# A transformer block on one core: the queue's products as halves of 64 rows between attention scores

## The chip, the cores and the metric

The kernel runs on one core of a Trainium2 chip. The metric is the device time of one launch in microseconds, inputs and outputs in the chip's main memory. Engines are called TensorE (PE), VectorE (DVE), ScalarE (ACT), GpSimd (POOL) and SyncE (SP, here the queue that issues transfers). TensorE's array has 128 rows by 128 columns. A matmul with 64 contraction rows uses half of the rows: rows 0 to 63 or rows 64 to 127, by where its operands lie. These halves are called row groups here.

## The reference

One post-norm transformer block over x of 4 x 2048 x 256, all in float32: attention with 16 heads of 16 and a full softmax, a residual and a layer norm, then a gated feed-forward of width 704 whose inputs and weights are rounded to FP4 in blocks of 16, a residual and a layer norm.

```python
scores = einsum('bhld,bhmd->bhlm', q, k) * SCALE
out = einsum('bhlm,bhmd->bhld', softmax(scores), v)
x = layernorm(x + out @ Wo.T)
h = silu(fp4_linear(x, w_gate)) * fp4_linear(x, w_up)
x = layernorm(x + fp4_linear(h, w_down))
```

## The kernel before, in words

**The periods.** The work is cut into steps (b, qb, g): one batch, a block of 512 queries, a group of 4 heads. There are 4 x 4 x 4 = 64 steps, and each runs over 16 key tiles of 128: 1,024 periods. The loop at the end of the kernel goes over periods `n`, from -`LEAD` (-20) to the last. In each it writes out instructions by a string, `ORDER`:

```python
ORDER = "m0 q m1 e0 e1 v e2 e3".split()
```

- `m0`, `m1` (`maxima`): scores of the step that is 20 periods ahead, for two heads each, queries on the output's partitions. Head j of the two lies on rows 64j to 64j+61, so its two matmuls use the two row groups. Both write one PSUM tile of two banks (`pm`), and one VectorE reduction over 128 x 1024 takes the row maxima of both heads (`mx`). After 16 periods `max_rows` turns the maxima and puts their negatives into the last rows of `q`, so that the scores below come out with the maximum subtracted.
- `e0` to `e3` (`exponentials`): the scores of one head and key tile, keys on the partitions, in one bank (`pe`), then ScalarE's exponential into SBUF (`e`, `E_BUFS` buffers).
- `v` (`values`): four matmuls `av`, each with 32 columns of weights (values and a column of ones), for the exponentials of two periods ago (`LAG`). Four such matmuls use the four column strips of the array side by side. At a step's end `normalize` divides by the sums.
- `q` (`more`): one part from a queue of other work: the projections of later blocks (`project`: `ptx` transposes, `pq`, `pv`), the weights' preparation (`prepare`), the output projection, and the feed-forward of the block that has just been attended (`feed_forward`: `py`, `ptq`, `pg`, `pu`, `pth`, `pz`), besides urgent parts of `max_rows` and `normalize` (`pn`, `pa`, `pr`). These parts are Python generators. A part is one PSUM bank's worth of matmuls or transposes and what reads it. Products have 128 contraction rows, and a float32 matmul appears as two rows of the trace; the scores' operands are of a rounded type and appear as one.

**Order.** TensorE's instructions (lines 148 and 151, through helpers) and VectorE's (line 83, `InOrder`) are kept in the order of the source. Whatever waits on TensorE (for a bank that VectorE or ScalarE still reads) stands in front of all that follows.

**PSUM.** There are eight banks: `ps_m` two tiles of two banks for maxima, `ps_av` one, `ps_x` three that exponentials and the queue's parts take in turn.

**Delays.** `later` and `take_due` do small VectorE and GpSimd steps (layer norm, FP4 rounding) a number of periods after they were asked for. A part whose data isn't ready by that count gives its period up.

**Ahead and after.** In the 20 periods ahead of the loop's start only maxima and two parts a period are written. The last block's feed-forward follows the loop in a version of its own (`feed_forward_last`).

Of the kernel before, what the change touches and what calls it, by code (L numbers as in the profile page):

```python
# [54 lines left out]
ORDER = "m0 q m1 e0 e1 v e2 e3".split()  # L56
E_BUFS = 10
LEAST = 300.0
# [17 lines left out]
class InOrder:  # L76
# [5 lines left out]
    def __getattr__(self, name):  # L82
        return lambda *args, **kw: self.tc.keep_in_program_order(getattr(self.engine, name)(*args, **kw))  # L83


@with_exitstack
def block_kernel(
# [25 lines left out]
    ps_m = ctx.enter_context(tc.tile_pool(name="ps_m", bufs=2, space=PSUM))  # L113
    ps_av = ctx.enter_context(tc.tile_pool(name="ps_av", bufs=1, space=PSUM))
    ps_x = ctx.enter_context(tc.tile_pool(name="ps_x", bufs=3, space=PSUM))


    banks = {"n": 0, "more": False}
# [31 lines left out]
    def transpose(*args):  # L150
        tc.keep_in_program_order(nc.tensor.transpose(*args))  # L151

# [107 lines left out]
    def turn_w(name, dst):  # L260
        for kc in range(KC):
            pt = psum("ptw")
            for n in range(KC):
                transpose(pt[:, n * P : (n + 1) * P], loaded[name][:, n, kc * P : (kc + 1) * P], ident)
            if name == "wv":
# [12 lines left out]

    RF = FF // 8

    def prepare():
# [5 lines left out]
        for kc in range(KC):  # L287
            for n in range(KC):
                at = (kc * KC + n) * P
                transpose(pt[:, at : at + P], raw[:, n, kc * P : (kc + 1) * P], ident)  # L290
        nc.scalar.copy(woT.rearrange("p k n -> p (k n)"), pt)
        yield 600
# [10 lines left out]
        def transposed(w, i, q, done):  # L303
            while not done():
                yield LEAST
            if w is w_down:
                q = q.rearrange("p b f -> p (b f)")
                for c0 in range(0, NFC, 4):
                    pt = psum("ptw")
                    for c in range(c0, min(c0 + 4, NFC)):  # L310
                        n = min(P, FF - c * P)
                        at = (c - c0) * P
                        transpose(pt[:n, at : at + P], q[:, c * P : c * P + n], ident)
                        nc.scalar.copy(wdT[:n, c, i * P : (i + 1) * P], pt[:n, at : at + P])
                return
            q = q.rearrange("p (c b) f -> p c (b f)", c=2)
            pt = psum("ptw")
            for kc in range(KC):
                for c in range(2):
                    at = (2 * kc + c) * RF  # L320
                    transpose(pt[:, at : at + RF], q[:, c, kc * P : (kc + 1) * P], ident[:RF, :RF])
# [3 lines left out]
            )  # L325

        pieces = [(w, i) for w in (w_gate, w_up) for i in range(4)] + [(w_down, i) for i in range(KC)]
        q = load(*pieces[0])
        yield 1
        for piece, after in zip(pieces, pieces[1:] + [None]):  # L330
# [3 lines left out]
            yield 600  # L334

    def weave(main, other, k):

        for cost in main:
            yield cost
            for _ in range(k if cost else 0):  # L340
                cost = next(other, None)
                if cost is None:
                    break
                yield cost
# [4 lines left out]
    def project(b, tb, what):  # L349
# [7 lines left out]
        for kc in range(KC):  # L357
            pt = psum("ptx")
            for t in range(QT):
                transpose(pt[:, t * P : (t + 1) * P], xb[:, t, kc * P : (kc + 1) * P], ident)  # L360
            nc.scalar.copy(xT[:, kc, :], pt)
            yield 600

        def q_or_k(name, c):
# [3 lines left out]
            for half in range(2):  # L368
                cols = slice(half * QB // 2, (half + 1) * QB // 2)
                pq = psum("pq")[:, : QB // 2]  # L370
                for kc in range(KC):
                    matmul(pq, w[:, kc, c * P : (c + 1) * P], xT[:, kc, cols], start=(kc == 0), stop=(kc == KC - 1))
                nc.scalar.copy(hi[:, cols], pq)
                nc.gpsimd.tensor_tensor(lo[:, cols], read(pq), hi[:, cols].bitcast(F32), ALU.subtract)
                yield 900
# [8 lines left out]
        def values_of():  # L384
            for t in range(QT):
                v = vt[(tb * 2 + t // 2) % 4]
                pv = psum("pv")
                for kc in range(KC):
                    matmul(
                        pv[:, :D], xT[:, kc, t * P : (t + 1) * P], wvT[:, kc, :], start=(kc == 0), stop=(kc == KC - 1)  # L390
                    )
# [11 lines left out]
                yield 900  # L403
# [35 lines left out]
    def maxima(s, n, i):  # L439

        if n == 0 and i == 0:
            mx_sb[s] = p2.tile([P, QT, HG, NQB], F32, tag="mx", name="mx")
        kb, t = n // QT, n % QT
        pm = ps_m.tile([P, 2, QB], F32, tag="pm", name="pm")
        for j in range(2):
            rows = slice(R * j, R * j + RM)
            matmul(
                pm[:, j, :],
                q_sb[s, i][rows, t * P : (t + 1) * P],
                k_sb[s, i, kb][rows, :],  # L450
                start=True,
                stop=True,
            )
        vector.tensor_reduce(mx_sb[s][:, t, 2 * i : 2 * i + 2, kb], pm, AX.X, ALU.max)

    def max_rows(s):
# [9 lines left out]
        for t in range(QT):  # L466
            transpose(
                pn[: 2 * HG, t * P : (t + 1) * P], nh[:, t].rearrange("p h c -> p (h c)").bitcast(F32), ident
            )
        nr = p2.tile([2 * HG, QB], F32R, tag="nr", name="nr", bufs=1)  # L470
        nc.scalar.copy(nr, pn[: 2 * HG, :])
        for i in range(NP):
# [5 lines left out]
        yield 400  # L478

    def exponentials(s, kt, h):  # L480
        i, j = divmod(h, 2)
        kb, col = kt // QT, kt % QT * P
        pe = psum("pe")
        rows = slice(R * j, R * j + R)
        matmul(pe, k_sb[s, i, kb][rows, col : col + P], q_sb[s, i][rows, :], start=True, stop=True)
        e = p1.tile([P, QB], F32, tag="e", name="e", bufs=E_BUFS)
        nc.scalar.activation(e, pe, AF.Exp, scale=SCALE)  # L487
        e_sb[s, kt, h] = e

    def values(s, kt):  # L490
        if kt == 0:
            av_ps[s] = ps_av.tile([P, QB], F32, tag="av", name="av")
# [11 lines left out]
    def normalize(s):  # L504
# [6 lines left out]
        for t in range(QT):  # L511
            transpose(pa[:, t * P : (t + 1) * P], av_sb[:, t * P : (t + 1) * P], ident)
# [14 lines left out]
        yield 600  # L527
        if s % 2 == 0:
            return
        yield 0  # L530
        pr = psum("pr")
        for t in range(QT):
            transpose(pr[:, t * P : (t + 1) * P], oq_of[s // 2][:, t, :], ident)
        oT = p1.tile([P, QB], F32, tag="oT", name="oT", bufs=3)
        nc.scalar.copy(oT, pr)
        oTs[s // 2] = oT
        yield 600
# [19 lines left out]
    def residual(b, qb, x1, xq):  # L557

        for t in range(QT):
            py = psum("py")  # L560
            for c in range(KC):
                matmul(
                    py[:, :D],
                    oTs[(b * NQB + qb) * KC + c][:, t * P : (t + 1) * P],
                    woT[:, c, :],
                    start=(c == 0),
                    stop=(c == KC - 1),
                )
            nc.gpsimd.tensor_add(x1[:, t, :], x1[:, t, :], read(py[:, :D]))
            if t % 2:  # L570
# [7 lines left out]
            yield 900  # L578

    def gated(xqT, h, t):  # L580
        for half in range(2):
            cols = slice(half * FH, (half + 1) * FH)
            pg = psum("pg")
            for kc in range(KC):
                matmul(
                    pg[:, :FH],
                    xqT[:, kc, t * P : (t + 1) * P],
                    wgT[:, kc, cols],
                    start=(kc == 0),
                    stop=(kc == KC - 1),  # L590
                )
# [4 lines left out]
            nc.scalar.activation(a, pg[:, :FH], AF.Tanh, scale=0.5)  # L596
            nc.gpsimd.tensor_mul(a, a, g)  # L597
            nc.gpsimd.tensor_add(a, a, g)  # L598
            yield 1200
            pu = psum("pu")  # L600
            for kc in range(KC):
                matmul(
                    pu[:, :FH],
                    xqT[:, kc, t * P : (t + 1) * P],
                    wuT[:, kc, cols],
                    start=(kc == 0),
                    stop=(kc == KC - 1),
                )
            u = p2.tile([P, FH], F32, tag="u", name="u")
            nc.scalar.copy(u, pu[:, :FH])  # L610
            nc.gpsimd.tensor_mul(h[:, cols], a, u)  # L611
            yield 1200

    def turned(hq, tiles, hT):
# [4 lines left out]
        for t in range(2):  # L619
            pt = psum("pth")  # L620
            for c in range(4):
                transpose(pt[:, c * P : (c + 1) * P], hq[t][:, c * P : (c + 1) * P], ident)
            nc.scalar.copy(hT[:, t, :4, :].rearrange("p c n -> p (c n)"), pt)
            yield 600
        pt = psum("pth").rearrange("p (t c n) -> p t c n", t=2, c=2)
        for t in range(2):
            for c in range(4, NFC):
                w = min(P, FF - c * P)
                transpose(pt[:w, t, c - 4, :], hq[t][:, c * P : c * P + w], ident)
        for c in range(4, NFC):  # L630
            w = min(P, FF - c * P)
            nc.scalar.copy(hT[:w, :, c, :], pt[:w, :, c - 4, :])
        yield 600

    def down(x1, hT, t):
        for n in range(KC):
            cols = slice(n * P, (n + 1) * P)
            pz = psum("pz")[:, :P]
            for c in range(NFC):
                w = min(P, FF - c * P)  # L640
                matmul(pz, hT[:w, t % 2, c, :], wdT[:w, c, cols], start=(c == 0), stop=(c == NFC - 1))
            nc.gpsimd.tensor_add(x1[:, t, cols], x1[:, t, cols], read(pz))  # L642
            yield 1300

    def feed_forward(b, qb, between):
# [9 lines left out]
        yield from islice(other, 7)  # L655
# [3 lines left out]
        for kc in range(KC):  # L659
            pt = psum("ptq")  # L660
            for t in range(QT):
                q = xq[t // 2][0].rearrange("p (t b) f -> p t (b f)", t=2)
                transpose(pt[:, t * P : (t + 1) * P], q[:, t % 2, kc * P : (kc + 1) * P], ident)
            nc.scalar.copy(xqT[:, kc, :], pt)
            yield 600
# [17 lines left out]
        yield from islice(other, 2)  # L683
        yield from gate(1)
        yield from islice(other, 2)
        yield from gate(2)
        yield from islice(other, 2)
# [18 lines left out]
    def feed_forward_last(b, qb, x1):  # L706
# [4 lines left out]

        def wide(name):
# [18 lines left out]
        def attended(t):  # L731
            py = psum("py")
# [11 lines left out]
        def up(t):  # L744
            pt = psum("ptq")[:, : KC * P].rearrange("p (k n) -> p k n", k=KC)
# [4 lines left out]
            for half in range(2):  # L750
                cols = slice(half * FH, (half + 1) * FH)
                pg, pu = psum("pg"), psum("pu")
# [22 lines left out]
        def downward(t):  # L775
# [3 lines left out]
            for c0 in range(0, NFC, 4):  # L779
                pt = psum("pth")  # L780
# [9 lines left out]
            pz = psum("pz")  # L790
# [183 lines left out]
```

## Time and profile before

| | |
|---|---|
| median of 3 runs | 3632.6 us (3631.36 to 3635.72) |
| the profiled execution | 3627.21 us, span 3625.4 us |
| granted TensorE clock, mean | 0.991 |
| TensorE matmul busy | 3531.5 us |
| VectorE busy | 2859.1 us |
| ScalarE busy | 2677.8 us |
| GpSimd busy | 1248.7 us |

The span is what the trace covers; the profiled execution's own time is 1.8 us over it, and the median 5.4 us over that. TensorE's row counts time in which some matmul's record is open; records overlap, since the next one starts to fetch while the last one still flows through the array. So the time between the starts of two rows tells more than a row's length. `PEld` are weight loads. In a line of the groups stand the engine, the operation, its tiles with shapes and the number of instructions, then the time busy in us, the mean length of one in ns, and the idle time just before them with what ended it.

### The profile page before, as it was taken

How to read it: one execution, taken by the hardware profiler on the slowest of the kernel's cores; microseconds unless marked ns; L12 is line 12 of the kernel's file. 1: busy time of each engine (PE TensorE's matmuls, PEld its weight loads, DVE VectorE, ACT ScalarE, POOL GpSimd, SP SyncE). 2: the span in 40 equal slices, each digit the busy share in tenths (PEclk: the TensorE clock that was granted, in tenths of full speed). 3: DMA queues.
4: the chain of work that ended last, by engine and by line, in shares of the span. 5: the costliest groups of instructions: out<-in, count | busy, mean ns of one | idle time of the engine just before them, and what ended most of it. 6: DMA issues, size and time to landing. Idle time of an engine off the chain costs nothing.

```text
span 3625.4 us, 57726 instructions
## 1 busy us (share of the span) xinstructions
PE 3531.5 (97%) x21348; PEld 1531.6 (42%) x21348; DVE 2859.1 (79%) x3310; ACT 2677.8 (74%) x5446; POOL 1248.7 (34%) x1496
## 2 busy tenths in 40 slices
PE   7889999999999999999999999999999999999997
PEld 5333444443444444444444444434444443434434
DVE  5777888788787877888788888887888788788845
ACT  3667777777777777777777777777777777777772
POOL 1232343423334332343333434333343433233341
PEclk9999999999999999999999999999999999999998
DMA  6533323232232322323223332322332222222200
GB/s 222 168 122 100 103 83 105 85 96 90 90 107 87 110 77 78 112 89 99 90 76 104 96 107 71 110 82 78 106 92 73 64 82 66 64 78 70 68 13 9
DMA packets 190640, 328.39 MB, mean 91 GB/s; under 512 B 24344, under 2 KB 68248, under 8 KB 190360
## 3 DMA queue, kind: packets, MB, share of 16 engines
q1 hardware_dynamic: 188968, 323.39, 29.5%
q8 instruction: 171, 2.80, 0.3%
q10 hardware_dynamic: 1392, 1.31, 0.1%
q14 instruction: 109, 0.89, 0.1%
HBM read 237.04 MB, written 86.51 MB: 89 GB/s over the span
## 4 chain that ended last, share of the span: by engine, by line
PE 88%; DVE 8%; DMA 2%; issue 1%; ACT 1%; SPq 0%; POOL 0%; POOLq 0%; ACTq 0%; DVEq 0%
PE av L148 25%; PE pe L148 19%; PE pm L148 17%; PE pz L148 6%; DVE mx L83 6%; PE pg L148 5%; PE pu L148 5%; PE pq L148 3%; PE pv L148 2%; PE py L148 2%; PE pth L151 1%; PE pa L151 1%; PE pn L151 1%; DVE m L83 1%; DMA wl<-in_L_ffn_w_gate_dram 1%
## 5 line engine op out<-in xcount | busy, mean ns | idle before, releaser
L83 DVE TENSOR_REDUCE mx<-pm 128x2 f32<-128x1024 f32 x2048 | 2456.6, 1221 | 617.9 <-PE pm L148 533.2
L487 ACT ACTIVATE e<-pe 128x512 f32<-128x512 f32 x4096 | 2216.0, 597 | 534.7 <-PE pe L148 522.0
L148 PE MATMUL av<-e,v 128*32 128x512 f32 x8192 | 1095.0, 607 | 3.3 <-DMA v<-vx 3.3
L148 PE MATMUL pe<-q,k 64*128 64x512 f32 x4096 | 1050.1, 458 | 3.7 <-ACT e L487 2.7
L148 PE MATMUL pm<-k,q 62*128 62x512 f32 x4096 | 934.2, 446 | 48.1 <-DVE mx L83 40.9
L148 PEld LDWEIGHTS pe<-q,k 64*128 64x128 f32 x4096 | 482.5, 185 | 947.7 <-ACT e L487 915.3
L148 PEld LDWEIGHTS pm<-k,q 62*128 62x128 f32 x4096 | 409.1, 186 | 339.6 <-DVE mx L83 179.0
L597 POOL TENSOR_TENSOR a<-a,g 128x352 f32<-128x352 f32 x120 | 112.3, 936 | 621.8 <-ACT a L596 621.7
L148 PEld LDWEIGHTS av<-e,v 128*32 128x32 f32 x8192 | 161.7, 108 | 330.0 <-issue 307.2
L178 POOL TENSOR_TENSOR xn<-xn,m 128x704 f32<-128x704 f32 (+2 forms) x100 | 153.3, 1533 | 249.1 <-DVE m L83 206.7
L148 PE MATMUL pz<-wdT,hT 128*128 128x128 f32 (+1 forms) x1488 | 230.6, 297 | 1.5 <-ACT hT L785 1.5
L148 PEld LDWEIGHTS pz<-wdT,hT 128*128 128x128 f32 x1488 | 188.9, 192 | 64.1 <-issue 43.4
L642 POOL TENSOR_TENSOR x<-x,read 128x128 f32<-128x128 f32 x120 | 55.0, 458 | 414.2 <-ACT read L156 404.0
L148 PE MATMUL pg<-wgT,xqT 128*128 128x352 f32 x512 | 186.6, 487 | 1.8 <-ACT xqT L748 1.8
L148 PE MATMUL pu<-wuT,xqT 128*128 128x352 f32 x512 | 185.7, 485 | 0.0
L611 POOL TENSOR_TENSOR h<-a,u 128x352 f32<-128x352 f32 x120 | 112.5, 938 | 138.5 <-ACT u L610 137.9
L179 POOL TENSOR_TENSOR xn<-xn,m 128x704 f32<-128x704 f32 (+2 forms) x100 | 153.3, 1533 | 7.2
L180 POOL TENSOR_TENSOR xn<-xn,sc 128x704 f32<-128x704 f32 (+2 forms) x100 | 126.2, 1262 | 6.4
L148 PEld LDWEIGHTS pg<-wgT,xqT 128*128 128x128 f32 x512 | 87.7, 190 | 75.0 <-issue 44.6
L148 PEld LDWEIGHTS pu<-wuT,xqT 128*128 128x128 f32 x512 | 88.0, 190 | 73.3 <-ACT e L487 37.3
L598 POOL TENSOR_TENSOR a<-a,g 128x352 f32<-128x352 f32 x120 | 114.8, 957 | 9.3
L156 ACT COPY read<-pz 128x128 f32<-128x128 f32 x120 | 31.8, 265 | 112.1 <-PE pm L148 103.6
(114 smaller groups left out, 2279.5 us busy)
## 6 DMA issues: line engine op xcount, KB each, us to landing
k<-kx SPq DMA_DIRECT2D x1024, 128.0 KB
v<-vx SPq DMA_DIRECT2D x64, 768.0 KB
q<-qx SPq DMA_DIRECT2D x256, 124.0 KB
kx<-khi SPq DMA_DIRECT2D x64, 256.0 KB
qx<-qhi SPq DMA_DIRECT2D x64, 256.0 KB
vx<-vt SPq DMA_DIRECT2D x32, 384.0 KB
xb<-in_L_attn_x_dram SPq DMA_DIRECT2D x16, 512.0 KB
kx<-klo SPq DMA_DIRECT2D x32, 256.0 KB
```

The costliest lines, as they stand in the source:

```text
L83: return lambda *args, **kw: self.tc.keep_in_program_order(getattr(self.engine, name)(*args, **kw))
L148: tc.keep_in_program_order(nc.tensor.matmul(*args, **kw))
L151: tc.keep_in_program_order(nc.tensor.transpose(*args))
L156: nc.scalar.copy(t, bank)
L178: nc.gpsimd.tensor_tensor(xn, xn, m, ALU.add)
L179: nc.gpsimd.tensor_tensor(xn, xn, m, ALU.subtract)
L180: nc.gpsimd.tensor_tensor(xn, xn, sc.unsqueeze(2).to_broadcast([p, nb, FB]), ALU.mult)
L487: nc.scalar.activation(e, pe, AF.Exp, scale=SCALE)
L597: nc.gpsimd.tensor_mul(a, a, g)
L598: nc.gpsimd.tensor_add(a, a, g)
L611: nc.gpsimd.tensor_mul(h[:, cols], a, u)
L642: nc.gpsimd.tensor_add(x1[:, t, cols], x1[:, t, cols], read(pz))
```

## The change

1. A product or a transpose of the queue is cut along its contraction rows: `product` and `turn` make a `Part`, a list of calls in which the upper ones (rows 64 to 127) come first and the lower ones (rows 0 to 63) follow. Both halves of a product add up in the same bank; a transpose's halves write 64 columns each. This holds while `split["on"]` is true, from period 0 until the maxima end.
2. The maxima are four steps a period instead of two: one matmul, one bank and one reduction over 128 x 512 for each head (`maximum`).
3. `ORDER` becomes a table with an order for each kind of part, "turn" (transposes), "square" (up to 256 output columns), "wide" (more), "long" (more than two contraction chunks) and "none". A step `u` issues the next upper call and a step `l` the next lower one. In each order all `u` come ahead of `v` and all `l` behind it, so a period's `l` and the next period's `u` stand in one stretch between two `v`.
4. The queue gives at most one part a period (`take_part`); urgent parts go first through `ready`.
5. PSUM banks are kept by number: three for maxima (four until period 0), one for `av`, four that exponentials and parts take from the head of a list and give back when what reads them has been written (`was_read`). The version for the last block goes round all eight.
6. `E_BUFS` is 11 instead of 10.

```diff
-ORDER = "m0 q m1 e0 e1 v e2 e3".split()
-E_BUFS = 10
+ORDER = {
+    "none": "e3 m1 e1 m2 v e2 m3 m0 e0",
+    "turn": "m3 u u u u e0 e2 m1 v m0 e3 e1 l m2 l l l",
+    "square": "u u e0 m2 e3 m0 v e2 m3 e1 l l m1",
+    "wide": "u m0 u e0 e2 m2 v e3 m3 e1 l m1 l",
+    "long": "u u m2 u u u e2 m0 v m3 e0 e1 e3 l l l l m1 l l",
+}
+FIRST = "m0 m1 m2 m3 q q"
+E_BUFS = 11
...
+    banks, banks_m, taken = deque(range(3)), deque(range(3, 7)), {}
+    def bank_of(i, name):
+        return ps.tile([P, 512], F32, tag=f"bank{i}", name=name)
     def psum(name):
-        banks["n"] += 1
-        if banks["more"] and banks["n"] % 2:
-            return ps_m.tile([P, 2, 512], F32, tag="pm", name=name)[:, 0, :]
-        return ps_x.tile([P, 512], F32, tag="px", name=name)
+        i = banks.popleft()
+        taken.setdefault(name, deque()).append(i)
+        return bank_of(i, name)
+    def was_read(name):
+        banks.append(taken[name].popleft())
...
+    def product(out, pairs):
+        kind = "long" if len(pairs) > 2 else "wide" if out.shape[1] > QB // 2 else "square"
+        def rows(h):
+            return [
+                (lhsT[r], rhs[r])
+                for lhsT, rhs in pairs
+                for r in [slice(h * R, min(h * R + R, lhsT.shape[0]))]
+                if r.start < r.stop
+            ]
+        upper = rows(1) if split["on"] else []
+        parts = upper + rows(0) if split["on"] else pairs
...
+    def turn(pairs):
+        calls, upper = [], 0
+        for h in (1, 0) if split["on"] else (None,):
+            for out, t in pairs:
+                n = t.shape[0]
+                r = slice(0, n) if h is None else slice(h * R, min(h * R + R, n))
+                calls.append(lambda out=out, t=t, r=r: transpose(out[:, r], t[r], ident[r, r]))
...
-        pm = ps_m.tile([P, 2, QB], F32, tag="pm", name="pm")
-        for j in range(2):
-            rows = slice(R * j, R * j + RM)
-            matmul(pm[:, j, :], q_sb[s, i][rows, ...], k_sb[s, i, kb][rows, :], ...)
-        vector.tensor_reduce(mx_sb[s][:, t, 2 * i : 2 * i + 2, kb], pm, AX.X, ALU.max)
+        bank = banks_m.popleft()
+        pm = bank_of(bank, "pm")
+        matmul(pm, q_sb[s, i][rows, t * P : (t + 1) * P], k_sb[s, i, kb][rows, :], start=True, stop=True)
+        vector.tensor_reduce(mx_sb[s][:, t, h : h + 1, kb], pm, AX.X, ALU.max)
+        banks_m.append(bank)
...
+        split["on"] = 0 <= n and m < N
+        part, g = take_part() if n >= 0 else (Part("none", []), None)
+        upper, lower = deque(part[: part.upper]), deque(part[part.upper :])
+        order = (ORDER[part.kind] if n >= 0 else FIRST).split()
+        for at, step in enumerate(order):
...
+            elif step == "u" and upper:
+                upper.popleft()()
+            elif (step == "l" or step == "q") and lower:
+                for _ in range(1 if part.upper else len(lower)):
+                    lower.popleft()()
+                if not lower:
+                    part_done(g)
```

More of the change, by code (lines that the diff above doesn't have):

```diff
@@ L333, in prepare, with some @@
             q = following
-            yield 600
-    def weave(main, other, k):
[L338 to L344, printed above, removed]
+    def some(parts, k):
+        while k > 0:
+            part = next(parts, None)
+            if part is None:
+                return
+            yield part
+            k -= part == LEAST
+    def weave(main, other, k):
+        for part in main:
+            yield part
+            if part == LEAST:
+                yield from some(other, k)
         yield from other
@@ L560, in residual @@
             py = psum("py")
[L561 to L568, printed above, removed]
+            yield product(
+                py[:, :D],
+                [(oTs[(b * NQB + qb) * KC + c][:, t * P : (t + 1) * P], woT[:, c, :]) for c in range(KC)],
+            )
             nc.gpsimd.tensor_add(x1[:, t, :], x1[:, t, :], read(py[:, :D]))
+            was_read("py")
             if t % 2:
@@ L583, in gated @@
             pg = psum("pg")
[L584 to L591, printed above, removed]
+            yield product(pg[:, :FH], [(xqT[:, kc, t * P : (t + 1) * P], wgT[:, kc, cols]) for kc in range(KC)])
             g = p2.tile([P, FH], F32, tag="g", name="g")
@@ L936, in block_kernel @@
                         queue.append(chain(*steps[s][:2]))
-    banks["more"] = True
-    while urgent or queue or due:
+        assert not upper and not lower
+        if m >= N:
+            take_due()
+    banks.extend([7])
+    while urgent or queue or due or ready:
         take_due()
-        more(1)
+        whole()
     feed_forward_last(*steps[-1][:2], x1_last)
```

272 lines of the change are left out of this document (152 added, 120 removed).

## The prediction

> **What bounds the kernel now.** I read the page's busy shares first, then its chain of waits, then the groups, and last the timeline of single periods.
>
> ```profile
> PE 3531.5 (97%) x21348; PEld 1531.6 (42%) x21348; DVE 2859.1 (79%) x3310; ACT 2677.8 (74%) x5446; POOL 1248.7 (34%) x1496
> ...
> PE 88%; DVE 8%; DMA 2%; issue 1%; ACT 1%; SPq 0%; POOL 0%; POOLq 0%; ACTq 0%; DVEq 0%
> ```
>
> TensorE is busy nearly always and carries the chain; VectorE is second. But a busy TensorE is not one that streams, so one period with a product between its scores comes next (TensorE's rows, start and length in us):
>
> ```profile
> 1000.13 1.07 PE L148 MATMUL av<-e,v 128*32 128x512 f32 x8
> 1001.12 0.50 PE L148 MATMUL pe<-q,k 64*128 64x512 f32 x2
> 1001.46 0.40 PE L148 MATMUL pm<-k,q 62*128 62x512 f32 x2
> 1001.79 1.13 PE L148 MATMUL py<-woT,oT 128*128 128x256 f32 x4
> 1002.85 0.50 PE L148 MATMUL pm<-k,q 62*128 62x512 f32 x2
> 1003.19 0.40 PE L148 MATMUL pe<-q,k 64*128 64x512 f32 x2
> 1003.52 1.06 PE L148 MATMUL av<-e,v 128*32 128x512 f32 x8
> ```
>
> The period is 1003.52 - 1000.13 = 3.39 us. Single rows inside `py` start at 1002.110, 1002.326, 1002.542: 0.216 us a step. A pair of scores, one head on rows 0-63 and one on 64-127, is one such step too. Yet the first pair of a stretch of 64 rows takes 0.34 (0.216 and 0.12 of weight load in the open), the second, before the form changes, 0.33 (0.216 and 0.11 until the array is empty); `py` takes 1.06 = 4 x 0.216 + 0.20. So eight steps stream 1.73 us, the `av` stretch lasts 0.99, and the rest is changes of form. Four forms follow each other here: `av`, 64 rows, 128 rows, 64 rows.
>
> **What TensorE gets from the change.** It leaves two forms: the product becomes 64-row halves, and a half on rows 64-127 can run beside a score on rows 0-63. Streaming does not shrink: eight steps on the whole array become 16 half-array steps, eight on each row group. What goes is the stretch of 128 rows: 0.20 for it and 0.23 for the second 64-row stretch. New period: 0.99 + 0.12 + 8 x 0.216 + 0.11 = 2.95, or 0.44 less; 1.22 of it is fixed.
>
> By the av groups in the trace there are 1,024 periods from 98.7 us to the end of the loop, 3446 us in all. By what stands between the scores I counted, with mean length: 132 with nothing (2.71 us), 318 with transposes (3.16), 216 with a product of up to 256 columns (3.45), 240 of 352 columns (3.70), 117 of the down projection (3.83). The same sum for each kind gives TensorE's new floor: nothing 1.22 + 4 x 0.216 = 2.09; transposes 1.22 + 0.86 + 4 x 0.109 (their step) = 2.52; 352 columns 1.22 + 0.86 + 4 x 0.295 = 3.27; the down projection, where rows 0-63 take 12 small matmuls at a step of 0.112, 1.22 + 0.86 + 12 x 0.112 = 3.43. The order strings balance the groups: in the "square" order rows 0-63 have e0, e2, m0, m2 and four matmuls of the l steps, rows 64-127 the same with u.
>
> **Whether the halves do run beside scores** is the step that all this rests on, since the new orders put two to five u steps in a row on one group. The down projection's last chunk has 64 rows, so before shows one such case:
>
> ```profile
> 1169.76 1.25 PE L148 MATMUL pz<-wdT,hT 128*128 128x128 f32 x8
> 1170.64 0.49 PE L148 MATMUL pm<-k,q 62*128 62x512 f32 x1
> 1170.85 0.27 PE L148 MATMUL pz<-wdT,hT 64*128 64x128 f32 x1
> 1170.88 0.48 PE L148 MATMUL pm<-k,q 62*128 62x512 f32 x1
> 1170.98 0.61 PE L148 MATMUL pe<-q,k 64*128 64x512 f32 x2
> ```
>
> In the program both `pz` come before both `pm`. A `pm` starts 0.21 us ahead of the last `pz`: the score on the free row group overtook it, and a `pe` of that group followed. Its semaphore, though, went up only after the earlier `pm` had ended, so results are signalled in program order. The row groups thus work down queues of their own; how deep one may run ahead of the other this trace shows for about five instructions, and the change needs up to twelve. The Trainium skill says the opposite ("TensorE: Matmul & The Clock Gate", Part 3, The mechanism): matmuls start and end strictly in program order, only weight loads are pulled ahead. By that rule the time would be the slow rival's below, 3765. I go by the row.
>
> **What VectorE pays.** Each maximum over two heads becomes two. The first row below is today's; the nearest row to the new one is `amax` over 512 elements (with shapes kept apart):
>
> ```profile
> L83 DVE TENSOR_REDUCE mx<-pm 128x2 f32<-128x1024 f32 x2048 | 2456.6, 1221 | 617.9 <-PE pm L148 533.2 <-PE pe L148 75.0
> ...
> L83 DVE TENSOR_REDUCE amax<-x 128x32 f32<-128x512 f32 x30 | 20.3, 677 | 0.0
> ```
>
> Where the next operation is ready it starts 0.085 us before such a row's end, so a reduction costs 1.136 today and 0.592 then: 4 x 0.592 = 2.37 a period against 2.27, +98 us over the run. At worst the shorter rows overlap nothing (4 x 0.677 = 2.71, +330 us); at best 512 elements cost half of 1.136 (no change). I take 0.592, a row of the same engine and width. VectorE's other work in the loop (statistics, quantization, reciprocals) sums to 325 us by rows, 0.32 a period: 2.69 in all. That is over TensorE's new floor in the periods with nothing or transposes, and 0.26 under it with squares. It comes in bursts: half the periods have none, a tenth over 0.87 us, and a burst stands in front of maxima in the queue, which TensorE's in-order waits turn into a stop. Three single banks for maxima (two double ones before) let VectorE lag by three reductions, 1.78 us; the `av` stretch with its change of form lasts 1.2, so it can be bridged.
>
> **The rest.** ScalarE keeps its instructions: four exponentials a period at a step of 0.49 and 0.38 of copies make 2.35, below every floor but near the transposes'; there a score waited for its bank in before (3.10 against 0.99 + 2 x 0.66 + 4 x 0.109 + 0.15 = 2.90). After, an exponential has three banks while a part holds the fourth, as many as now, but a part's bank no longer stands in their rotation; I count this as nothing, at worst the same 0.19 in 318 periods, 60 us. Halved transposes double the instructions but not the time: four steps on each group side by side instead of four on the whole array; if a half's weight load could not run beside the other's, +0.44 in 318 periods, 139 us (bounded above by the rows' 0.109 step; the `pz` and `pe` weight loads of 1170.74 and 1170.75 do run together, so I take none). POOL (34%), the DMA queues (30% of their time) and SP issue the same transfers, in the same periods; hidden as now. E_BUFS 11 adds one buffer of lead: nothing. The prologue keeps whole products and grows by 20 x 0.1 = 2 us; the tail gets eight banks in a ring: 0 to -5.
>
> **The sum.** Mean period after = the larger of TensorE's floor and VectorE's 2.69, with an allowance for bursts, chosen larger where VectorE binds:
> - nothing: 132 x 2.74 = 362 (before 358)
> - transposes: 318 x 2.82 = 897 (1006)
> - up to 256 columns: 216 x 3.08 = 665 (744)
> - 352 columns: 240 x 3.38 = 811 (889)
> - down: 117 x 3.53 = 413 (449)
>
> Together 3148; some 25 us of early waits for transfers, which the means before hold, stay: 3173 against 3446, or -273. From the profiled execution's 3627 that gives 3354. Its allowances are 0.05 to 0.13 a period (some 100 us in all); bursts that land badly cost more than they spare, so I add 16: 3370, and 3375 with the 5 us by which the median (3632.6) stands above the profiled one. About 0.2% is what a measurement of this kernel can tell from no change.
>
> **The rivals.**
> - *VectorE idles between bunches* (0.18). Today it waits 618 us before maxima, 0.60 a period, while TensorE is at other work. If 0.45 of that stays because maxima still arrive in bunches on either side of `av`, the 666 periods without wide products take 2.69 + 0.45 = 3.14: 2091 + 811 + 413 + 25 = 3340, 106 saved, 3526. For it: order strings with both last maxima just ahead of `v`. Against it: four separate signals and three banks.
> - *The groups do not run ahead of each other* (0.10), slower. With starts in program order, "u u e0" lets e0 start only with the last of four matmuls. By steps of 0.216 the square order then needs 11 instead of 8, 3.60 against 3.39; 352 columns 13.2 steps, 4.08; down 14.4, 4.34; transposes 8, 2.96. Against before: +46, +89, +57, -45, and -13 in empty periods: +134, 3765. It decides if more than some 0.43 a period of group time stands empty, which is the gain. Against it: the overtaking `pm`.
> - *The run-ahead is short* (0.10). Half of the u steps run alone, two of the eight steps: -0.44 + 0.43, no gain, and VectorE's +98 us partly shows: 3630 to 3700.
>
> **How the numbers follow.** The main case (0.62) spans 3265 (nearly all allowances gone: 3354 - 100 and the 5 of the median, rounded up) to 3450 (TensorE's floors and the copies' and transposes' worst bounds by half). The first rival fills 3450 to 3590. Range 3265 to 3590: 0.60 + 0.17 is inside, and the slow cases lie outside. Faster: 0.62 + 0.18 + 0.02 of the last; slower: 0.10 + 0.06; same 0.02.
>
> **What would show it.** Right: period lengths by kind near the list; one stretch of 64-row rows between two `av` stretches; u rows and e or m rows of different groups starting together; maxima of 512 elements near 677 ns; VectorE near 88% busy. Wrong: a score that starts only when the last u of its run has started (strict order), VectorE idle before maxima at 0.4 a period or more (bunches), reductions above 0.7 us, or transposes with 0.2 a step.

## The result and the profile after

The changed kernel takes 3635.7 us in the median of 20 runs (3630.3 to 3641.2), the kernel before 3629.8 us (3627.1 to 3635.7) beside it: ratio 1.0015, 95% interval 1.0008 to 1.0022. That is inside the 0.2% called no change above, and 261 us over the forecast of 3375. From the first `av` group to the last, the loop takes 3451 us against 3446 before and 3173 in the forecast's sum.

The page of the changed kernel: span, busy shares, the chain's shares, and the two groups that VectorE and ScalarE work at most.

```profile
span 3636.6 us, 68397 instructions
...
PE 3453.1 (95%) x25532; PEld 1868.8 (51%) x25532; DVE 3011.1 (83%) x5358; ACT 2627.8 (72%) x5446; POOL 1249.1 (34%) x1496
...
PE 77%; DVE 14%; ACT 4%; DMA 2%; issue 1%; POOL 0%; SPq 0%; POOLq 0%; ACTq 0%; DVEq 0%
...
L95 DVE TENSOR_REDUCE mx<-pm 128x1 f32<-128x512 f32 x4096 | 2592.6, 683 | 494.7 <-PE pm L173 243.7
L567 ACT ACTIVATE e<-pe 128x512 f32<-128x512 f32 x4096 | 2227.1, 601 | 855.8 <-PE pe L173 374.8
```

TensorE's share of the chain fell from 88% to 77%; VectorE's rose from 8% to 14%, ScalarE's from 1% to 4%. Something was taken from TensorE, and other waits came in its place. That the first half is true is seen in one stretch with 352 columns (TensorE's rows). In the program its order is pe, pm, pe, pg, pm, pg, pu, pm, pu, pe, pe, pm, where each pg and each pu is a call of two rows.

```profile
1943.47 0.50 PE L173 MATMUL pe<-q,k 64*128 64x512 f32 x1
1943.48 0.56 PE L173 MATMUL pg<-wgT,xqT 64*128 64x352 f32 x1
1943.81 0.39 PE L173 MATMUL pm<-k,q 62*128 62x512 f32 x1
1943.88 0.46 PE L173 MATMUL pg<-wgT,xqT 64*128 64x352 f32 x1
1944.04 0.40 PE L173 MATMUL pe<-q,k 64*128 64x512 f32 x1
...
1945.00 0.40 PE L173 MATMUL pe<-q,k 64*128 64x512 f32 x1
1945.11 0.45 PE L173 MATMUL pu<-wuT,xqT 64*128 64x352 f32 x1
1945.24 0.40 PE L173 MATMUL pe<-q,k 64*128 64x512 f32 x1
1945.41 0.46 PE L173 MATMUL pu<-wuT,xqT 64*128 64x352 f32 x1
```

The first `pg` starts at 1943.48, ahead of the `pm` and the second `pe` that are written before it; the `pe` of 1945.00 starts ahead of both rows of the second `pu`, which is written before it. So the row groups do run down queues of their own, and there is one stretch of 64 rows between two `av` groups instead of three stretches.

What came in its place stands in the waits (engine, tile and line, what it waited for: us in total, times, longest):

```profile
PEld pe L173 <- ACT e L567: 569.9, 977, 1.5
PEld pm L173 <- DVE mx L95: 426.7, 689, 5.6
DVE mx L95 <- PE pm L173: 243.7, 432, 3.6
PE pr L176 <- DVE oq L95: 60.8, 32, 2.7
```

The totals of the first two lines must be read with care. The first weight load behind an `av` group counts as waiting, 0.84 us each time, while the `av` matmuls still run, and that costs nothing. Taken apart row by row, 466 of the 569.9 us are of this sort and 258 of the 426.7 (858 of 915.3 and none of 179.0 before). What is left rose from 58 to 104 us for `pe`, which wait until ScalarE has read a bank, and went from 179 to 169 us for `pm`, which wait for a reduction. A load that waits while the other row group still loads is in neither figure, so the experiments below have to say what the waits cost. VectorE's wait for `pm` fell from 533.2 to 243.7 us. The last line is new.

I measured the stretches between two `av` groups. Each now holds the `l` half of one part and the `u` half of the next; the table has those in which both are of one kind. Floor and forecast are the prediction's; the other columns are measured, in us. "Before" is the mean of the whole period with such a part. The number of stretches is that of the changed kernel; "nothing" takes in two at the end, where the maxima run out. The four columns on the right are experiments below.

| kind | before, mean | floor | forecast | after, mean (median) | e1_gap, median | e5_gap_short, median | e6_exp_half, median | e10_both_short, median |
|---|---|---|---|---|---|---|---|---|
| nothing (82) | 2.71 | 2.09 | 2.74 | 3.04 (2.77) | 2.75 | 2.47 | 2.75 | 2.47 |
| transposes (163) | 3.16 | 2.52 | 2.82 | 3.49 (3.19) | 3.14 | 3.14 | 2.77 | 2.71 |
| up to 256 columns (118) | 3.45 | 2.95 | 3.08 | 3.16 (3.10) | 3.10 | 3.10 | 3.00 | 3.00 |
| 352 columns (164) | 3.70 | 3.27 | 3.38 | 3.37 (3.33) | 3.33 | 3.33 | 3.34 | 3.34 |
| down (73) | 3.83 | 3.43 | 3.53 | 3.68 (3.68) | 3.68 | 3.67 | 3.68 | 3.67 |

Products of 352 columns gave what was forecast. Transposes, a third of all parts, became longer than they were, and so did the mean with nothing. (The mean with transposes takes in 31 stretches of 4.76 us, the subject of the first experiment.)

### The profile page after: what moved, and what is told of

The parts are those of the page before. It is cut to its first block, busy times and chain, and to the rows that moved or that the text cites. A ratio compares the mean times of both kernels' runs of the same rounds, so it can differ in the third digit from the quotient of the medians.

```text
span 3636.6 us, 68397 instructions
## 1 busy us (share of the span) xinstructions
PE 3453.1 (95%) x25532; PEld 1868.8 (51%) x25532; DVE 3011.1 (83%) x5358; ACT 2627.8 (72%) x5446; POOL 1249.1 (34%) x1496
## 3 DMA queue, kind: packets, MB, share of 16 engines
q8 instruction: 204, 3.34, 0.4%
q10 hardware_dynamic: 1392, 1.31, 0.1%
## 4 chain that ended last, share of the span: by engine, by line
PE 77%; DVE 14%; ACT 4%; DMA 2%; issue 1%; POOL 0%; SPq 0%; POOLq 0%; ACTq 0%; DVEq 0%
PE av L173 25%; PE pe L173 17%; PE pm L173 15%; DVE mx L95 9%; PE pz L173 5%; PE pg L173 4%; PE pu L173 4%; ACT e L567 3%; PE pq L173 3%; DVE m L95 2%; PE pv L173 2%; PE py L173 1%; DMA q<-qx 1%; PE pth L176 1%; DVE st L95 1%
## 5 line engine op out<-in xcount | busy, mean ns | idle before, releaser
L95 DVE TENSOR_REDUCE mx<-pm 128x1 f32<-128x512 f32 x4096 | 2592.6, 683 | 494.7 <-PE pm L173 243.7
L173 PE MATMUL pm<-k,q 62*128 62x512 f32 x4096 | 1719.5, 464 | 52.9 <-DVE mx L95 34.8
L173 PE MATMUL pe<-q,k 64*128 64x512 f32 x4096 | 1639.2, 455 | 2.9 <-DVE oq L95 1.1
L173 PEld LDWEIGHTS pm<-k,q 62*128 62x128 f32 x4096 | 738.9, 187 | 571.4 <-DVE mx L95 426.7
L173 PEld LDWEIGHTS pe<-q,k 64*128 64x128 f32 x4096 | 694.5, 186 | 652.8 <-ACT e L567 569.9
L173 PE MATMUL pg<-wgT,xqT 64*128 64x352 f32 (+1 forms) x984 | 350.8, 473 | 13.0 <-ACT xqT L728 11.2
L173 PE MATMUL pu<-wuT,xqT 64*128 64x352 f32 (+1 forms) x984 | 350.2, 473 | 0.0
L173 PE MATMUL pz<-wdT,hT 64*128 64x128 f32 (+2 forms) x2608 | 308.7, 280 | 5.8 <-ACT hT L694 4.1
L173 PEld LDWEIGHTS pz<-wdT,hT 64*128 64x128 f32 (+1 forms) x2608 | 297.7, 189 | 18.6 <-ACT hT L694 6.4
L173 PEld LDWEIGHTS pu<-wuT,xqT 64*128 64x128 f32 (+1 forms) x984 | 173.2, 187 | 17.5 <-issue 1.7
```

The lines of the kernel that those rows point to most:

```text
L173: tc.keep_in_program_order(nc.tensor.matmul(*args, **kw))
```

## The experiments

Three theories stood for the missing 261 us. *A wait at the queue's head*: the diff drops a `yield 0` in `normalize`, so that `pr`, which needs what VectorE makes of `pa`, now follows `pa` at once. *VectorE's pace*: single-head maxima cost more of the path than the 98 us of busy time that I mostly hid. *The exponentials' banks*: a cut part keeps its bank from its first `u`, over `v`, to the read after its last `l`. Two parts then hold banks at once in nearly every stretch, and the four exponentials go round the two or three that are left. A fourth, that the halves or their orders bring nothing, was the rival to all of them.

**The wait at the queue's head.** The timeline of the changed kernel, one period with `pa` and then `pr`:

```profile
1515.08 1.29 DVE L95 TENSOR_REDUCE mx<-pm 128x1 f32<-128x512 f32 x2 [0.38 <-PE pa L176]
...
1515.23 0.34 PE L176 MATMUL pa<-ident,av_sb 64*128 64x64 f32 x3
1516.29 0.25 DVE L95 RECIPROCAL rd<-pa 128x16 f32<-128x16 f32 x1
1516.57 0.49 DVE L95 TENSOR_TENSOR oq<-pa,rd 128x128 f32<-128x128 f32 x2
...
1517.20 0.24 PE L176 MATMUL pr<-ident,oq 64*128 64x64 f32 x1 [1.63 <-DVE oq L95]
```

The last `pa` row ends at 1515.57. VectorE first finishes two maxima that stand ahead in its queue, then makes reciprocal and products. The first `u` of `pr` stands in the same stretch, behind the last `l` of `pa`; it waits 1.63 us, and every score of the next period that is written behind it waits too. Such stretches take 4.76 us in the mean, 31 of them. e1_gap puts the empty period back:

```diff
         if s % 2 == 0:
             return
+        yield 0
         pr = psum("pr")
```

> The changed kernel with one period of other work between the transposes pa and pr of normalize, as the kernel before had it. Theory A (part of TensorE's gain is lost because a u step stands at the front of TensorE's queue and waits for VectorE's result of the part just ahead): the 31 periods that hold pa and pr fall from 4.76 us to about 2.9, so about 55 us less, 3580. Theory B (VectorE sets the pace anyway, whatever TensorE waits for): less than 15 us, because the wait only moves.

Measured: 3575.3 us, ratio to the kernel before 0.9851 (0.9836 to 0.9865), 60 us less than the changed kernel. The line `PE pr <- DVE oq` is gone from its waits. This theory holds, for 60 of the 261 us, and the kernel of this run is faster than both of the case. Not all of the 60 is the wait itself. Around 16 of the 31 waits the changed kernel's trace shows the granted TensorE clock at half, for 3.4 us each time but one: behind the `pr` above, the clock is 0.63 from 1518 to 1522 us and 1.00 in the next four, and the `av` group of 1518.09 takes 1.93 us where others take 1.07. The stretch behind such a wait lasts 4.46 us in the mean, against 3.15 behind the other 15, which makes an estimate of 16 x 1.31 = 21 us. Between 350 and 3000 us neither the kernel before nor e1_gap has a stretch at half clock. Two waits of the same kind are left in e1_gap's trace: 9 `ptx` followed by `pq` (4.08 us, where transposes and then squares have a median of 3.14) and 13 `ptq` followed by `pg` (4.08; transposes and then 352 columns 3.37), some 18 us by the trace alone; no run took these away.

**The halves.** e2_whole leaves all products and transposes whole, with the new orders, banks and maxima:

```diff
-        split["on"] = 0 <= n and m < N
+        split["on"] = False
```

> The changed kernel with products and transposes left whole (128 rows), issued at the first l step; banks, orders and single-head maxima as changed. If the halves do save TensorE the 0.2 to 0.4 us a part period that the trace after shows (352 columns 3.37 against 3.70, down 3.68 against 3.83, squares 3.16 against 3.45), this kernel loses them again: 150 to 200 us slower than the changed kernel, 3790 to 3830. If the halves bring nothing because row groups do not overlap, it is within 30 us of 3636.

Measured: 4004.7 us, 1.1036 (1.1019 to 1.1052), above what was expected. Stretches with 352 columns took 4.37 us, down 4.25, though before, with the same whole products in the old order, they took 3.70 and 3.83. So the run shows that the rest of the change needs the halves, but not what the halves alone are worth: with whole products the new orders cost much of this themselves. e9_turn_whole asks the narrower question, on top of e1_gap, with only the transposes whole:

```diff
-        for h in (1, 0) if split["on"] else (None,):
+        for h in (None,):
```

> e1_gap with transposes left whole (128 rows, all four at the first l step) and products in halves. Theory C: transposes in halves gain TensorE nothing, because their periods are held by the exponentials' banks (3.14 us, against a floor of 2.52); whole ones take their bank for a shorter time: between 3540 and 3600, no loss. If halves are worth the change of form for transposes too (0.38 us in some 300 periods): about 100 us slower, 3680.

Measured: 3627.0 us, 0.9987 (0.9978 to 0.9997), 52 us over e1_gap, between what the two theories expected. By this run halved transposes are worth 0.16 us in each of 318 periods, so they are not the fault; but they are worth less than the forecast's 0.34. As in e2_whole, the whole ones stand in orders made for halves, so even 0.16 may be partly the order's.

**VectorE's pace.** e3_short reduces only half of each row (256 of 512 columns) and so makes VectorE's part short; e5_gap_short does this to e1_gap.

```diff
-        vector.tensor_reduce(mx_sb[s][:, t, h : h + 1, kb], pm, AX.X, ALU.max)
+        vector.tensor_reduce(mx_sb[s][:, t, h : h + 1, kb], pm[:, : QB // 2], AX.X, ALU.max)
```

> The changed kernel with each maximum taken over 256 of the 512 columns: the same instructions, banks and waits, VectorE's reduction about 0.27 us shorter. (The maxima of the other columns are left out.) Theory B (VectorE's pace and its bunched maxima set the periods with nothing, transposes and squares): those fall towards TensorE's floors, 150 to 250 us less, 3390 to 3490. Theory A (data waits at the head of the queue): only the share of DVE in the waits for pa and pr, less than 40 us. Theory C (ScalarE and its banks): less than 30 us.

> e1_gap with each maximum taken over 256 of the 512 columns (the maxima of the other columns are left out). If the wait of pa and pr and VectorE's pace are two separate losses, they add up, less the 19 us by which e3_short already shortened the pa and pr periods: 3575 - 120 = 3455. If VectorE's pace only showed because of those waits, it stays above 3540.

Measured: 3497.5 us for e3_short, 0.9637 (0.9623 to 0.9651), 138 us less than the changed kernel and just above what was expected; 3458.0 us for e5_gap_short, 0.952 (0.9506 to 0.9534), 117 us less than e1_gap, as expected. In the table e5_gap_short takes 0.28 from the median with nothing, and nothing from the medians of the other kinds; their means lose up to 0.04, and the mean of the 50 stretches with squares and then transposes falls from 3.52 to 3.26. The weight loads for `pm` that wait elsewhere than right behind an `av` group wait 52 us, against 169 in e1_gap. So VectorE's pace costs 117 to 138 us at the most, where periods are short and where bursts of its other work come: e3_short takes 975 us of busy time from VectorE, much more than the 152 us that the change had added. e8_before_single asks whether single-head maxima cost this in the old kernel as well (four single banks for them):

```diff
-    ps_m = ctx.enter_context(tc.tile_pool(name="ps_m", bufs=2, space=PSUM))
+    ps_m = ctx.enter_context(tc.tile_pool(name="ps_m", bufs=4, space=PSUM))
...
-        pm = ps_m.tile([P, 2, QB], F32, tag="pm", name="pm")
...
+            pm = ps_m.tile([P, QB], F32, tag="pm", name="pm")
...
-        vector.tensor_reduce(mx_sb[s][:, t, 2 * i : 2 * i + 2, kb], pm, AX.X, ALU.max)
+            vector.tensor_reduce(mx_sb[s][:, t, 2 * i + j : 2 * i + j + 1, kb], pm, AX.X, ALU.max)
```

> The kernel before with nothing changed but the maxima: one bank and one reduction over 128 x 512 for each head, four single banks. If VectorE's extra 98 us of reductions are hidden as long as TensorE sets the pace, it is within 25 us of 3630, and the periods with nothing between (2.6 us, held by the two double banks) may shorten a little. If single-head maxima cost time by themselves, it is 60 to 130 us slower.

Measured: 3643.0 us, 1.0031 (1.002 to 1.0042): 11.5 us more. Only the periods with nothing are longer (2.79 against 2.71); 352 columns and down stay at 3.70 and 3.83. Its waits for the same two tiles:

```profile
PEld pe L148 <- ACT e L487: 908.7, 1207, 1.7
...
DVE mx L83 <- PE pm L148: 438.4, 862, 6.0
```

VectorE still waits 438 us for `pm` here: its extra 116 us of busy time lie under TensorE's. In the changed kernel part of the same instructions lies in the open: in the stretches with nothing on either side VectorE is busy for 2.92 of 3.07 us, and with 352 columns for 2.76 of 3.37. But the changed kernel also has three banks for maxima where e8_before_single has four, and this run doesn't separate the two.

**The exponentials' banks.** The timeline of the changed kernel, a stretch with transposes on both sides (an `av` group at 2235.04 and the next at 2238.18, 3.14 us; its floor is 2.52):

```profile
2236.61 1.08 ACT L567 ACTIVATE e<-pe 128x512 f32<-128x512 f32 x2 [0.52 <-PE pth L176]
2236.73 0.52 PE L176 MATMUL pth<-ident,xn 64*128 64x64 f32 x7
2237.26 0.18 PEld L173 LDWEIGHTS pe<-q,k 64*128 64x128 f32 x1 [0.15 <-ACT e L567]
...
2237.58 0.59 ACT L687 COPY hT<-pth 128x512 f32<-128x512 f32 x1
2237.75 0.18 PEld L173 LDWEIGHTS pe<-q,k 64*128 64x128 f32 x1 [0.30 <-ACT e L567]
```

Two exponentials come behind `v` (`e3`, `e1`) and two in front of the next (`e0`, `e2`). Both of the latter wait, 0.15 and 0.30 us, until ScalarE has read the former: `pth` and the part after it hold the other banks. ScalarE itself isn't full: it was idle for 0.52 us until the first score of the stretch was there, and its four exponentials and one copy then take about 2.4 of the 3.14 us. What binds is that the last two scores have no bank to go to until two exponentials have been made. e4_fourbanks gives the bank that changes sides at period 0 back to the maxima, so that these have four and exponentials and parts three:

```diff
-        if n == 0:
-            banks.append(banks_m.popleft())
```

> The changed kernel with four banks for maxima throughout and three for exponentials and parts (instead of three and four). If maxima in bunches of four per 64-row stretch are held by three banks, the periods with nothing between fall from about 2.74 to 2.5 and the time by 20 to 60 us. If exponentials need the fourth bank (a part holds one for a whole period), the time rises by 50 us or more.

Measured: 4049.6 us, 1.116 (1.1141 to 1.1179), 414 us more than the changed kernel. The wait for ScalarE, of which 199 us now stand elsewhere than right behind an `av` group (104 in the changed kernel):

```profile
PEld pe L173 <- ACT e L567: 690.0, 1022, 1.0
```

The mean with nothing falls from 3.04 to 2.80 us, since VectorE has one more bank to lag by; the whole loss lies in the stretches with parts. e6_exp_half goes the other way, on top of e1_gap: exponentials of half of the columns, so that a bank is read sooner (the other half of each `e` holds ones).

```diff
-        nc.scalar.activation(e, pe, AF.Exp, scale=SCALE)
+        nc.scalar.activation(e[:, : QB // 2], pe[:, : QB // 2], AF.Exp, scale=SCALE)
```

> e1_gap with ScalarE's exponentials over 256 of the 512 columns (the other columns of e hold ones; that part of the exponentials is left out). Same instructions and banks; ScalarE's step falls from 0.49 to about 0.28 us. Theory C (a split part holds its bank from its first u over v to the read after its last l, so exponentials are left two or three banks, and a score waits for ScalarE to read the one before): periods with transposes on both sides fall from 3.14 towards 2.8, the time by 80 to 150 us, 3425 to 3495. If ScalarE and its banks do not matter: less than 30 us.

Measured: 3494.0 us, 0.9619 (0.9603 to 0.9635), 81 us less than e1_gap, the least gain that was expected. The same wait:

```profile
PEld pe L173 <- ACT e L575: 453.7, 549, 0.8
```

985 such waits in e1_gap became 549, and those elsewhere than right behind an `av` group, 446 with 111 us in e1_gap, became 10 with 2 us. The median with transposes fell from 3.14 to 2.77 us; with nothing it stays at 2.75. The two theories thus act on different periods: VectorE's pace on those with nothing, the exponentials' banks on those with transposes and, by 0.10, on those with up to 256 columns. A shorter exponential shortens ScalarE's work as well as the time for which a bank is held. That a bank and not ScalarE's work is what binds rests on e4_fourbanks and on ScalarE's 2.4 us of work in stretches of 3.14; no run frees a bank alone.

**Both together.** e10_both_short has the edits of e1_gap, e3_short and e6_exp_half.

> e1_gap with both cuts: maxima over 256 columns and exponentials over 256 columns (the rest of both is left out). If VectorE's pace (117 us) and the exponentials' banks (81 us) are separate losses, they add: 3575 - 198 = 3377, about the time that was forecast without them. If one hides behind the other, it stays above 3420.

Measured: 3336.2 us, 0.9188 (0.9173 to 0.9204), 239 us less than e1_gap, where the two alone gave 117 + 81 = 198. Its page and two groups with shapes kept apart:

```profile
PE 3221.1 (96%) x25532; PEld 1831.3 (55%) x25532; DVE 2027.6 (61%) x5358; ACT 1847.2 (55%) x5446; POOL 1250.2 (37%) x1507
```

```profile
L95 DVE TENSOR_REDUCE mx<-pm 128x1 f32<-128x256 f32 x4096 | 1601.2, 420 | 1154.4 <-PE pm L173 595.2 <-PE pe L173 127.9 <-PE pth L176 61.7
...
L575 ACT ACTIVATE e<-pe 128x256 f32<-128x256 f32 x4096 | 1384.5, 386 | 1176.1 <-PE pe L173 403.8 <-PE pm L173 373.4 <-PE pth L176 71.6
```

With both out of the way, VectorE and ScalarE idle over 1100 us each in front of these rows, and TensorE mostly sets the pace: with up to 256 and with 352 columns the medians are 3.00 and 3.34 over floors of 2.95 and 3.27, with transposes 2.71 over 2.52. With nothing they stay at 2.47 over 2.09; in the stretch from 567.39 the last maximum still waits 0.28 us for one of its three banks. The time is 39 us below the forecast and less than either case expected. That fits the forecast's picture of TensorE, but it is no test of its sum, which counted whole reductions and exponentials.

**Orders.** If banks are what binds, a different place for the exponentials should help. e11_turn_three (on e1_gap) puts three of them behind `v` for transposes, e12_all_three in all orders but that of the down projection (that is, "none", "turn", "square", "wide"):

```diff
-    "turn": "m3 u u u u e0 e2 m1 v m0 e3 e1 l m2 l l l",
+    "turn": "m3 u u u u e0 m1 v e2 e3 m0 e1 l m2 l l l",
```

> e1_gap with the order for transposes changed to 'm3 u u u u e0 m1 v e2 e3 m0 e1 l m2 l l l': three exponentials behind v and one ahead of it, instead of two and two; each group's work in a stretch stays the same. Theory C: scores that start as the stretch begins find three banks at rest, only the fourth waits, and periods with transposes on both sides fall from 3.14 to 2.8 or less: 20 to 60 us less than 3575. If the order of exponentials does not matter: within 15 us.

> As e11_turn_three, and the orders for nothing, squares and 352 columns also have three exponentials behind v and one ahead of it, so that every stretch has four exponentials whatever parts meet in it. Theory C: 40 to 100 us less than 3575. Against: exponentials bunched behind v make ScalarE idle ahead of it, and the maxima come later in the stretch: slower than e11_turn_three.

Theory C missed in both, in sign too: 3615.0 us, 0.9958 (0.9943 to 0.9973), 40 us more than e1_gap, and 3698.1 us, 1.0191 (1.0175 to 1.0207), 123 us more, slower than e11_turn_three as the argument against it had said. The median with transposes on both sides falls from 3.14 to 3.10 us, but where transposes are followed by squares it rises from 3.14 to 3.59, and followed by 352 columns from 3.37 to 3.82. Such a mixed stretch has five exponentials in e11_turn_three, three behind `v` and the two that the next part's old order still has ahead of it. Three exponentials in a row behind `v` are three turns of ScalarE; the first `u` of the next part, or the exponential after it, then finds no free bank. In e12_all_three squares go from 3.10 to 3.57 and 352 columns from 3.33 to 3.56. The wait was moved, not removed, by these two orders; no others were tried. A fifth bank for exponentials and parts was not tried either: all eight are given out (three, one and four).

## Why the prediction was wrong

**TensorE's terms: right, but for one size.** One stretch instead of three, rows of different groups side by side, and 352 columns at 3.37 us against a forecast of 3.38. Up to 256 columns came to 3.16 against 3.08, with a median of 3.10 that fell to 3.00 where exponentials are short, so little of this is TensorE's. The rival of strict order (3765) is refuted by the first `pg` and the second `pu` above. The rule of the Trainium skill that matmuls start and end strictly in program order ("TensorE: Matmul & The Clock Gate", Part 3, The mechanism) does not hold for two row groups here: the `pe` of 1945.00 starts 0.11 us ahead of a `pu` that is written before it. The rival of a short run-ahead names 3630 to 3700, and the time fell there by luck; its cause is refuted by the same rows, and by stretches with 352 columns at a median of 3.33 over a floor of 3.27. The down projection's floor was too low: 3.67 to 3.68 us in all five kernels of the table, whatever VectorE and ScalarE did, against 3.53; its cause inside TensorE stays open, at 0.15 x 117 = 18 us. The floors were summed as if both sides of a stretch were of one kind, and in 403 of 1003 they are not. That did no harm: counted from the program's order for each row group, with its own scores, the floors add up to about 2850 us against 2842, and in e10_both_short 352 columns followed by transposes have a median of 2.93 us, near the 2.95 of that count. Two slips in the prediction's bounds changed no forecast. VectorE's worst case, 4 x 0.677 against 2 x 1.136, is 446 us and not 330. And the strict-order rival took 3.39 and 3.10 for means that its own list gives as 3.45 and 3.16; with those it comes to about 3740.

**A wait for which the sum has no term.** I read the queue's parts as parts whose data is ready and never looked at who makes it. The dropped `yield 0` put `pr` right behind `pa` with VectorE's queue in between: 60 us (e1_gap), some 21 of them, by the estimate above, the half clock that followed.

**"What VectorE pays": the row was right, the cover was not.** The reduction steps 0.598 us where one is queued (0.592 taken), and VectorE's busy time rose by 152 us against 98. Periods with nothing have a median of 2.77 us, forecast 2.74. What failed is "an allowance for bursts": I set 0.05 to 0.13 a period, some 100 us in all, and with nothing the mean is 3.04 where 2.74 was forecast. Shortening the maxima recovers 117 us, which bounds what a larger allowance could have been. The first rival, VectorE idle between bunches, is not refuted. All idle time before maxima fell only from 617.9 to 494.7 us, 0.48 a period, and the prediction's sign for this rival was 0.4 or more. Yet little of it lies where VectorE sets the pace: it is 0.13 us a stretch with nothing on both sides, 0.35 with transposes and 0.38 with up to 256 columns, against the rival's 0.45, and 0.66 with 352 columns. What it costs apart from the pace, no run shows.

**"I count this as nothing": the exponentials' banks.** This is the step that failed most plainly. I saw the sentence that decides it, that a part's bank no longer stands in the rotation, and priced it at 0, at worst 60 us, because three banks sounded like as many as now. But two cut parts overlap in a stretch, so there are at times only two, and stretches with transposes on both sides came to a median of 3.14 us (e1_gap) against the 2.82 that was forecast. Halved exponentials, which also shorten ScalarE's work, give 81 us back alone; with VectorE's pace out of the way too, 239 - 117 = 122.

**The sum.** 60 for the queue's head and 239 for the two others together are 299 us, against 261 that were missing. So these three are enough to cover the shortfall. They are not an account of it to the microsecond: halved rows save work that the forecast had counted as well as the waits, and how the 198 of single effects and the 41 of joint effect spread over the periods is not taken apart.

## What to carry to other kernels

Work that is cut in two parts around a fixed point holds its bank, its buffer, for the whole way between; count the banks at the fullest place of the cycle, not on the average. When a floor is lowered by 0.4 us a period, list for each period what has lain under the old one, and what is late next: here three waits, each worth some 60 to 140 us in the runs that shortened or removed it, were enough to take back the whole gain. A total of waits is not a cost either: look at what else runs during each. An empty slot in a hand-written order may be there for data: before it is filled, find who makes what the next step reads and what is queued ahead of that.

## What the runs showed of the hardware

The two row groups overtake each other by whole calls: a `pg` written behind two scores of the other group started 0.33 and 0.56 us before them. Behind 16 of 31 waits of the changed kernel the granted clock stood at half for 3.4 us or more, and an `av` group took 1.93 us in place of 1.07. Halving a reduction's width saves less than half of its time: a row has 683 ns for 512 columns and 420 for 256. And moving one of four banks from the exponentials and parts to the maxima cost 414 us, three times the 138 us that halved reductions gave on the same kernel.
